# A block's values by way of DRAM, and another order of a turn, in a recurrent megakernel

## The chip, the cores and the metric

The kernel runs on one core of one Trainium2 chip. The metric is device time in microseconds of one execution, the median of several runs. A core has five engines that work side by side, each through its own instructions in order: TensorE (PE, matmuls and transposes into PSUM; PEld is its weight load), VectorE (DVE), ScalarE (ACT), GpSimd (POOL) and SyncE (SP), which here issues nearly all DMAs. They wait for each other only through semaphores.

## The reference

The input is 16 sequences of 256 tokens with 128 features. It is normalized, and goes two ways that meet at the end, `out = x + s * silu(g)`:

- `s`: a small state-space layer. Two convolutions of four taps, a softplus step size, and a scan over the 256 tokens for each of 16 states, `h = dA * h + d * u * B`, `y = sum over states of h * C`, then a projection.
- `g`: six layers, each of an attention and a feed-forward part with residuals. Both read the tokens with half of the features shifted by one token.

```python
def attn_layer(x, Wqkv, qs, ksc, Wo):          # 16 heads of 64
    q, k, v = split(x @ Wqkv)
    q = l2norm(q) * qs;  k = l2norm(k) * ksc
    q = q * cos * scale + rotate_half(q) * sin * scale
    k = k * cos / scale + rotate_half(k) * sin / scale
    # windows of 32 queries: each sees its own 32 keys and the 32 before them
    sim  = einsum(bq, look(bk)) * 8;  sim = where(mask, -big, sim)
    out  = einsum(softmax(sim), look(bv))
    return out @ Wo

def ffn_layer(x, g, bln, W1, b1, W2, b2):      # 128 -> 2 * 341 -> 128
    a, gate = split((layernorm(x) * g + bln) @ W1 + b1)
    return (a * gelu(gate)) @ W2 + b2
```

The diff bears on `look(bv)`: to each window of 32 queries belong 64 rows of values, its own 32 and the 32 before, so that each row of values is wanted in two places.

## The kernel before

Activations stay in SBUF in fp32 as `xT` (features on partitions). Attention works in blocks of 128 tokens: 2 blocks per sequence (`blk` 0 and 1), 32 per layer, 192 over the six layers. A block passes through a pipeline, and a program loop takes one **turn** per block. In turn `n` the tuple `order` is walked, and a pair `(step, ahead)` works on block `n + ahead`: `project 4` projects q and k of block `n + 4`, `scale 2` and `turn 2` normalize and transpose those of block `n + 2`, `score 1`, `greatest 1`, `subtract 1`, `soften 1` and `values 1` make the softmax's numerators and the values of block `n + 1`, and `turn_weights 0`, `attend 0`, `divide 0`, `turn_out 0` finish block `n`. `close` applies Wo to a whole sequence, in two halves of 8 matmuls: the first at the end of an odd turn, the second in the next even one. `guess`, `refine`, `close` and `residual` run for odd blocks only.

Into these turns other work is fed:

- `feed` advances the feed-forward part of an earlier group of four blocks by one step, three times in a turn; a group of 512 tokens takes four turns. By n mod 4: turn 1 transposes the tokens and takes row statistics (L162 and L163 on VectorE, `rstd` on GpSimd), turn 2 normalizes (GpSimd's `less`, four ScalarE activations) and transposes back, turn 3 runs 12 hidden matmuls (L359) with gelu, turn 0 the 6 of the second product (L382) and two residual adds (L385). After the last layer, `end` closes a group in a turn 0: silu on ScalarE, a product on VectorE, 4 transposes (L411), a sum, the output's DMA.
- `state` advances the scan by one of 16 states: `decay` (ScalarE exp), `drive` (GpSimd), `advance` (VectorE scan, L298), `weigh` (GpSimd, two products) and `bring` (on SP, the DMA that broadcasts two rows of 512 for the state after next, 512 KB; its three buffers make it wait for `weigh` of the same turn). A group of 512 tokens takes 20 turns; all eight are through by about turn 165. `prepare` computes the next group's inputs, `norms_on` the first normalization of later groups.

The order of the instructions on each engine is the order of the program (`manual_schedule`). So a step late in `order` that waits on its engine holds up all steps behind it on that engine, in the next turn too. The framework puts in the semaphores: for data, and for reuse of a buffer.

PSUM is one tile of 8 banks of 512 floats; `where` gives each step's first bank. A name read by `pair` takes two banks, one read by `bank` takes one: pairs are q, k, v, qT, kT, s (scores), w (transposed weights), av (attention results of heads 0 to 6), o (its transposes), h0 to h2 (hidden products); single banks are e and l (results of the last heads), pw (Wo), f and n.

The values: `values` projects them into PSUM, and `hand_out` copies them with ScalarE into `vt` (L490), 128 tokens by 2 x 8 heads of 65 floats, the 65th of each head being 1, for the softmax's denominator. From there DMAs on SP place each window's 64 rows in `v2`, one copy per parity `r` of the head, and `attend` multiplies by those rows:

```python
nc.tensor.matmul(
    b["pav7"][r][jj, 0:VW] if c == 7 else b["pav"][jj, r, c, :],
    aT[rr, c, jj],
    v2[rr, j, c * VW : (c + 1) * VW], ...
```

`attend` starts with the pair of heads 7, whose results lie in banks e and l, and `divide_last` divides them; `divide` divides the rest.

Of the kernel before, what the change touches and what calls it, by code (L numbers as in the profile page):

```python
# [8 lines left out]
FP = mybir.dt.float32  # L9
# [6 lines left out]
B, L, DM = 16, 256, 128  # L16
NT = B * L
DEPTH = 6
H, DH, W = 16, 64, 32
NP = H // 2  # L20
# [6 lines left out]
VW = DH + 1  # L27
# [3 lines left out]
def tile_kernel(ctx: ExitStack, tc: tile.TileContext, a, out):  # L31
    nc = tc.nc
# [4 lines left out]
    p = ctx.enter_context(tc.tile_pool(name="at", bufs=1))  # L37
    ff = ctx.enter_context(tc.tile_pool(name="ff", bufs=1))
    mb = ctx.enter_context(tc.tile_pool(name="mb", bufs=1))
    far = ctx.enter_context(tc.tile_pool(name="far", bufs=2, space=bass.MemoryType.DRAM))  # L40
    pst = ctx.enter_context(tc.tile_pool(name="pst", bufs=1, space=PSUM))


    where = dict(q="6", k="0", v="4", qT="4", kT="0", s="2", w="4", av="2", o="2", h0="6", h1="0", h2="4", e="7", l="6", pw="4", f="7", n="1")
    psum = pst.tile([128, 8, G], FP, name="psum")

    def pair(name):
# [369 lines left out]
    blocks = [dict(layer=n // BL, s=n % BL // NB, blk=n % NB) for n in range(DEPTH * BL)]  # L417

    vts = [const.tile([128, 2, NP, VW], FP, name=f"vt{i}") for i in range(NB)]
    v2s = [const.tile([128, 4, NP * VW], FP, name=f"v2{i}") for i in range(NB)]  # L420
    kTs = [const.tile([128, NP, W + L], FP, name=f"kT{i}") for i in range(2)]
    for t in vts:
        nc.gpsimd.memset(t[:, :, :, DH : DH + 1], 1.0)
    for o in (0, 64):
        nc.gpsimd.memset(v2s[0][o : o + W, 0, :], 0.0)
    for t in kTs:
        nc.gpsimd.memset(t[:, :, 0:W], 0.0)

# [56 lines left out]
    def hand_out(n):  # L485
        b = blocks[n]
        blk, pq = b["blk"], b["pv"]

        vt = vts[blk]
        nc.scalar.copy(  # L490
            vt[:, :, :, 0:DH].rearrange("p r c d -> p c r d"),
            pq.rearrange("p (c r d) -> p c r d", c=NP, r=2),
        )
        vt = vt.rearrange("p r c d -> p r (c d)")

        v2 = v2s[blk]
        for r in range(2):
            o = r * 64
            if blk:
                before = vts[blk - 1].rearrange("p r c d -> p r (c d)")  # L500
                nc.sync.dma_start(out=v2[o : o + W, 0, :], in_=before[96:128, r, :])
            nc.sync.dma_start(out=v2[o + W : o + 64, 0, :], in_=vt[0:W, r, :])
            for j in range(1, 4):
                nc.sync.dma_start(
                    out=v2[o : o + 64, j, :], in_=vt[W * (j - 1) : W * (j + 1), r, :]
                )

    def lengths(n, i):
# [252 lines left out]
    def feed():  # L761
# [5 lines left out]


    order = (
        (norms_on, None),  # L770
        (lengths, 3, 1),
        (guess, 3),
        (close, -1, 1),
        (residual, -1),
        (feed, None),
        (project, 4, 0),
        (prepare, None),
        (score, 1),
        (rotate, 4, 0),
        (turn_weights, 0),  # L780
        (rotate2, 4, 0),
        (greatest, 1),
        (state, None, weigh),
        (refine, 3),
        (subtract, 1),
        (scale, 2, 0),
        (turned_weights, 0),
        (project, 4, 1),
        (square, 4, 0),
        (state, None, bring),  # L790
        (values, 1),
        (scale, 2, 1),
        (add, 4, 0),
        (rotate, 4, 1),
        (state, None, decay),
        (hand_out, 1),
        (rotate2, 4, 1),
        (add, 4, 1),
        (attend, 0),
        (divide_last, 0),  # L800
        (state, None, drive),
        (turn, 2, 0),
        (divide, 0),
        (state, None, advance),
        (square, 4, 1),
        (lengths, 4, 0),
        (turned_q, 2),
        (feed, None),
        (feed, None),
        (state, None, put_out),  # L810
        (turn_out, 0),
        (turned_out, 0),
        (turn, 2, 1),
        (turned_k, 2),
        (close, 0, 0),
        (soften, 1),
    )
    last = DEPTH * BL - 1
    with tc.manual_schedule():
# [125 lines left out]
```

## Time and profile before

| | us |
|---|---|
| median of 3 runs | 3457.33 |
| lowest and highest | 3450.86, 3460.79 |
| the profiled execution's own time | 3454.1 |
| its span, first to last instruction | 3452.3 |

| engine | busy, us | share |
|---|---|---|
| PE | 3280.4 | 95% |
| DVE | 2758.3 | 80% |
| POOL | 2592.6 | 75% |
| ACT | 2135.5 | 62% |

The DMA engines moved 305 MB, 88 GB/s; their packets took 33.1% of the time of 16 engines on SP's queue. The mean granted TensorE clock was 0.987. In lists of groups and of the timeline, a line names the start, the duration, the engine, the kernel's line (L437), the operation, what is written and read, and in brackets how long the engine stood idle before, and who released it.

### The profile page before, as it was taken

Reading aid. Unit: us, or ns where it says so; the run is one execution under the profiler, and the core shown is the slowest. Engines: PE = TensorE matmul, PEld = TensorE weight load, DVE = VectorE, ACT = ScalarE, POOL = GpSimd, SP = SyncE. Lnnn points to the kernel's source line nnn. Section 1 sums busy time; section 2 is a strip of 40 time slices with the busy share of each in tenths; the row PEclk is TensorE's granted clock in tenths of the full one; section 3 lists DMA queues with packets and bytes.
Section 4 is the critical chain, followed back from the end, with each engine's and each line's share of the span. In section 5 each row is a group of like instructions: output and inputs, shape, how many; then the busy total and the mean of one; then the engine's idle time right before and its main releaser. Section 6 shows DMA issues by size and latency. Waiting matters only on the chain.

```text
span 3452.3 us, 139990 instructions
## 1 busy us (share of the span) xinstructions
PE 3280.4 (95%) x62176; PEld 2186.9 (63%) x62176; DVE 2758.3 (80%) x3642; ACT 2135.5 (62%) x2741; POOL 2592.6 (75%) x2362
## 2 busy tenths in 40 slices
PE   7999999999999999999999999999999999999996
PEld 3666666666666666666666666666666666666664
DVE  6787878887888788878977898778979887677663
ACT  4666666665766576657655666566656666656654
POOL 6688858885888689868986798679968996555550
PEclk9999999999999999999999999999999999999998
DMA  3434333433333333333333333334323332222221
GB/s 93 109 92 107 82 81 99 103 85 82 103 94 92 90 101 96 84 85 91 108 87 88 91 99 88 86 94 100 96 76 98 98 100 70 69 62 67 69 66 56
DMA packets 191850, 305.03 MB, mean 88 GB/s; under 512 B 32719, under 2 KB 58637, under 8 KB 191245
## 3 DMA queue, kind: packets, MB, share of 16 engines
q1 hardware_dynamic: 190956, 295.74, 33.1%
q8 instruction: 489, 8.01, 1.0%
q14 instruction: 117, 0.95, 0.1%
q10 hardware_dynamic: 288, 0.33, 0.0%
HBM read 95.33 MB, written 8.91 MB: 30 GB/s over the span
## 4 chain that ended last, share of the span: by engine, by line
PE 79%; DVE 8%; ACT 5%; issue 3%; POOL 3%; DMA 0%; SPq 0%; DVEq 0%; POOLq 0%; ACTq 0%
PE psum L437 25%; PE psum L562 14%; PE psum L718 10%; PE psum L667 8%; PE psum L359 7%; PE psum L611 6%; PE psum L382 3%; ACT oT L566 3%; DVE o L691 2%; PE psum L597 2%; PE psum L231 2%; DVE hs L298 1%; DVE t L469 1%; DVE ss L514 1%; POOL t L480 1%
## 5 line engine op out<-in xcount | busy, mean ns | idle before, releaser
L480 POOL TENSOR_TENSOR t<-t,t 128x1024 f32<-128x1024 f32 x384 | 958.8, 2506 | 359.6 <-DVE den L683 210.3
L437 PE MATMUL psum<-wqkv,xT 128*128 128x512 f32 x2304 | 1067.8, 599 | 9.0 <-ACT aT L566 5.0
L552 POOL TENSOR_TENSOR t<-t,y 128x1024 f32<-128x1024 f32 x384 | 722.6, 1903 | 7.5
L437 PEld LDWEIGHTS psum<-wqkv,xT 128*128 128x128 f32 x2304 | 418.3, 192 | 391.7 <-issue 308.7
L458 DVE TENSOR_TENSOR t<-psum,tab 128x1024 f32<-128x1024 f32 x384 | 468.4, 1220 | 161.4 <-PE psum L437 150.7
L566 ACT COPY aT<-psum 128x1024 f32<-128x1024 f32 x192 | 194.3, 1012 | 563.9 <-PE psum L562 563.9
L469 DVE TENSOR_TENSOR t<-psum,tab 128x1024 f32<-128x1024 f32 x384 | 466.4, 1215 | 0.0
L514 DVE TENSOR_REDUCE ss<-sq 128x16 f32<-128x1024 f32 x384 | 456.6, 1199 | 1.3
L562 PE MATMUL psum<-ident,t 128*128 128x128 f32 x3072 | 412.6, 277 | 21.8 <-issue 9.8
L667 PEld LDWEIGHTS psum<-v,aT 64*32 64x32 f32 x24576 | 295.2, 105 | 177.2 <-issue 127.3
L448 ACT ACTIVATE sq<-psum 128x1024 f32<-128x1024 f32 x384 | 394.9, 1028 | 15.5 <-DVE t L469 10.8
L718 PE MATMUL psum<-oT,wo 128*128 128x256 f32 x1536 | 357.5, 386 | 24.2 <-ACT oT L566 24.1
L562 PEld LDWEIGHTS psum<-ident,t 128*128 128x128 f32 x3072 | 340.2, 141 | 43.4 <-issue 14.1
L667 PE MATMUL psum<-v,aT 64*32 64x65 f32 x24576 | 331.8, 227 | 26.2 <-issue 24.6
L718 PEld LDWEIGHTS psum<-oT,wo 128*128 128x128 f32 x1536 | 283.8, 190 | 81.7 <-ACT oT L566 47.0
L490 ACT COPY vt<-psum 128x1024 f32<-128x1024 f32 x192 | 196.1, 1022 | 203.6 <-PE psum L437 203.6
L611 PEld LDWEIGHTS psum<-kT,qT 64*32 64x32 f32 x24576 | 283.9, 105 | 12.1 <-issue 1.7
L611 PE MATMUL psum<-kT,qT 64*32 64x64 f32 x24576 | 287.6, 226 | 2.2 <-issue 2.2
L566 ACT COPY oT<-psum 128x1024 f32<-128x1024 f32 x192 | 195.3, 1017 | 129.8 <-PE psum L562 127.2
L298 DVE TENSOR_TENSOR_SCAN hs<-dA,bc 128x512 f32<-128x512 f32 x128 | 271.5, 2121 | 0.0
L624 DVE TENSOR_REDUCE top<-psum 128x16 f32<-128x1024 f32 x192 | 233.4, 1216 | 46.3 <-PE psum L611 46.2
L359 PE MATMUL psum<-xn,w 128*128 128x512 f32 (+1 forms) x576 | 264.0, 609 | 5.5 <-ACT o L684 4.6
(104 smaller groups left out, 4601.2 us busy)
## 6 DMA issues: line engine op xcount, KB each, us to landing
v<-vt SPq DMA_DIRECT2D x1152, 130.0 KB, 2.4
bc<-rows SPq DMA_DIRECT2D x128, 512.0 KB, 5.1
v<-vt SPq DMA_DIRECT2D x576, 65.0 KB, 2.7
wqkv<-in_Wqkv SPq DMA_DIRECT2D x18, 512.0 KB, 6.5
wo<-in_Wo SPq DMA_DIRECT2D x6, 512.0 KB, 4.2
first<-in_x SPq DMA_DIRECT2D x8, 256.0 KB, 5.0
xn<-xT SPq DMA_DIRECT2D x16, 128.0 KB, 2.7
pad<-xn SPq DMA_DIRECT2D x8, 256.0 KB
```

Source lines behind the costliest of these rows:

```text
L359: nc.tensor.matmul(ph[0:n, i * G : (i + 1) * G], w1[:, i * DI + c0 : i * DI + c0 + n], xn, start=True, stop=True,)
L437: nc.tensor.matmul(pq[:, cc], xb, wq[:, cc], start=True, stop=True)
L458: nc.vector.tensor_tensor(t1.rearrange("p (h d) -> p h d", h=H), b["pq", i].rearrange("p (h d) -> p h d", h=H), table(n, i, 0).unsqueeze(1 ...
L469: nc.vector.tensor_tensor(t2.rearrange("p (h f d) -> p h f d", h=H, f=2), b["pq", i].rearrange("p (h f d) -> p h f d", h=H, f=2)[:, :, ::- ...
L480: nc.gpsimd.tensor_tensor(b["qk", i], b["qk", i], b["t2", i], ALU.add)
L514: nc.vector.tensor_reduce(b["ss"][:, j * H : (j + 1) * H], b["sq", i].rearrange("p (h d) -> p h d", h=H), AX.X, ALU.add,)
L552: nc.gpsimd.tensor_tensor(t3, t3, b["inv"][:, j * H : (j + 1) * H].unsqueeze(2).to_broadcast([128, H, DH]), ALU.mult,)
L562: nc.tensor.transpose(pt[:, cc], of[:, cc], ident)
L566: nc.scalar.copy(to, pt.rearrange("p (c t) -> p c t", c=NP))
L611: nc.tensor.matmul(sc4[jj, r, c, :], qT[rr, c, jj], kT[rr, c, k0 : k0 + 64], start=False, stop=True, skip_group_check=True,)
L667: nc.tensor.matmul(b["pav7"][r][jj, 0:VW] if c == 7 else b["pav"][jj, r, c, :], aT[rr, c, jj], v2[rr, j, c * VW : (c + 1) * VW], start=Tru ...
L718: nc.tensor.matmul(b["pw"][:, 0:L], wo[:, c, :], b["oT"][:, c, :], start=(c == 0), stop=(c == NP - 1), skip_group_check=True,)
```

## The change

It does three things.

- `hand_out` no longer places the windows from `vt`. It writes the block's 128 rows of values, as they are, to a DRAM tile (`vds`, one of two, for even and odd sequences) with one DMA of 520 KB. Ahead of each sequence's first row lie 32 rows of zeros, written once.
- A new step `windows` reads them back into `v2` with four DMAs of 260 KB, for each parity of heads and each half of a window one: 32 partitions by 4 windows by 2080 bytes. It stands at the head of a turn, for the block that the same turn attends.
- `order` is another, and `where` gives other banks. On TensorE the turn was: second half of close, q projection, score, turn_weights, k projection, values, attend, turn q, feed, turn_out, turn k, first half of close. It becomes: turn_weights, second half of close, q projection, score, values, k projection, attend, turn k, turn q, turn_out, feed, first half of close.

```diff
--- before.py
+++ after.py
@@ -41,7 +41,7 @@
     pst = ctx.enter_context(tc.tile_pool(name="pst", bufs=1, space=PSUM))
 
 
-    where = dict(q="6", k="0", v="4", qT="4", kT="0", s="2", w="4", av="2", o="2", h0="6", h1="0", h2="4", e="7", l="6", pw="4", f="7", n="1")
+    where = dict(q="6", k="2", v="0", qT="4", kT="0", s="4", w="2", av="6", o="6", h0="0", h1="2", h2="4", e="4", l="5", pw="0", f="1", n="3")
     psum = pst.tile([128, 8, G], FP, name="psum")
 
     def pair(name):
@@ -421,8 +421,11 @@
     kTs = [const.tile([128, NP, W + L], FP, name=f"kT{i}") for i in range(2)]
     for t in vts:
         nc.gpsimd.memset(t[:, :, :, DH : DH + 1], 1.0)
-    for o in (0, 64):
-        nc.gpsimd.memset(v2s[0][o : o + W, 0, :], 0.0)
+
+    vds = [far.tile([W + L, 2, NP * VW], FP, name=f"vd{i}", bufs=1) for i in range(2)]
+    nc.gpsimd.memset(v2s[0][0:W, 0:2, :], 0.0)
+    for t in vds:
+        nc.sync.dma_start(out=t[0:W], in_=v2s[0][0:W, 0:2, :])
     for t in kTs:
         nc.gpsimd.memset(t[:, :, 0:W], 0.0)
 
@@ -491,18 +494,22 @@
             vt[:, :, :, 0:DH].rearrange("p r c d -> p c r d"),
             pq.rearrange("p (c r d) -> p c r d", c=NP, r=2),
         )
-        vt = vt.rearrange("p r c d -> p r (c d)")
-
-        v2 = v2s[blk]
+
+
+        rows, t0 = vds[b["s"] % 2], blk * 128
+        nc.sync.dma_start(out=rows[W + t0 : W + t0 + 128], in_=vt.rearrange("p r c d -> p r (c d)"))
+
+    def windows(n):
+        b = blocks[n]
+        rows, v2, t0 = vds[b["s"] % 2], v2s[b["blk"]], b["blk"] * 128
         for r in range(2):
-            o = r * 64
-            if blk:
-                before = vts[blk - 1].rearrange("p r c d -> p r (c d)")
-                nc.sync.dma_start(out=v2[o : o + W, 0, :], in_=before[96:128, r, :])
-            nc.sync.dma_start(out=v2[o + W : o + 64, 0, :], in_=vt[0:W, r, :])
-            for j in range(1, 4):
+            for half in range(2):
+                o = r * 64 + half * W
                 nc.sync.dma_start(
-                    out=v2[o : o + 64, j, :], in_=vt[W * (j - 1) : W * (j + 1), r, :]
+                    out=v2[o : o + W],
+                    in_=rows[t0 + half * W : t0 + half * W + 128, r].rearrange(
+                        "(j k) x -> k j x", k=W
+                    ),
                 )
 
     def lengths(n, i):
@@ -767,53 +774,54 @@
 
 
     order = (
+        (windows, 0),
+        (turn_weights, 0),
+        (close, -1, 1),
+        (turned_weights, 0),
+        (project, 4, 0),
+        (lengths, 3, 1),
+        (state, None, decay),
+        (prepare, None),
         (norms_on, None),
-        (lengths, 3, 1),
         (guess, 3),
-        (close, -1, 1),
         (residual, -1),
         (feed, None),
-        (project, 4, 0),
-        (prepare, None),
+        (rotate, 4, 0),
+        (rotate2, 4, 0),
+        (state, None, put_out),
         (score, 1),
-        (rotate, 4, 0),
-        (turn_weights, 0),
-        (rotate2, 4, 0),
+        (square, 4, 0),
         (greatest, 1),
+        (values, 1),
+        (refine, 3),
+        (project, 4, 1),
+        (scale, 2, 1),
+        (hand_out, 1),
+        (scale, 2, 0),
+        (subtract, 1),
+        (attend, 0),
+        (turn, 2, 1),
+        (soften, 1),
+        (divide_last, 0),
+        (rotate, 4, 1),
+        (divide, 0),
+        (add, 4, 0),
+        (square, 4, 1),
+        (rotate2, 4, 1),
+        (turn, 2, 0),
+        (turned_k, 2),
         (state, None, weigh),
-        (refine, 3),
-        (subtract, 1),
-        (scale, 2, 0),
-        (turned_weights, 0),
-        (project, 4, 1),
-        (square, 4, 0),
-        (state, None, bring),
-        (values, 1),
-        (scale, 2, 1),
-        (add, 4, 0),
-        (rotate, 4, 1),
-        (state, None, decay),
-        (hand_out, 1),
-        (rotate2, 4, 1),
+        (turn_out, 0),
+        (turned_out, 0),
+        (state, None, advance),
+        (state, None, drive),
         (add, 4, 1),
-        (attend, 0),
-        (divide_last, 0),
-        (state, None, drive),
-        (turn, 2, 0),
-        (divide, 0),
-        (state, None, advance),
-        (square, 4, 1),
+        (turned_q, 2),
         (lengths, 4, 0),
-        (turned_q, 2),
         (feed, None),
         (feed, None),
-        (state, None, put_out),
-        (turn_out, 0),
-        (turned_out, 0),
-        (turn, 2, 1),
-        (turned_k, 2),
+        (state, None, bring),
         (close, 0, 0),
-        (soften, 1),
     )
     last = DEPTH * BL - 1
     with tc.manual_schedule():
```

## The prediction

> **What bounds the kernel now.** I read the page's busy times and chain first.
>
> ```profile
> PE 3280.4 (95%) x62176; PEld 2186.9 (63%) x62176; DVE 2758.3 (80%) x3642; ACT 2135.5 (62%) x2741; POOL 2592.6 (75%) x2362
> PE 79%; DVE 8%; ACT 5%; issue 3%; POOL 3%; DMA 0%; SPq 0%; DVEq 0%; POOLq 0%; ACTq 0%
> ```
>
> TensorE is busy 95% of the span and carries 79% of the chain; DMA carries 0% of it. The list of TensorE's own waits shows how little could be gained:
>
> ```profile
> PE psum L411 <- DVE xn L407: 39.1, 8, 6.0
> PE psum L718 <- ACT oT L566: 24.1, 95, 1.1
> ```
>
> (Total us, times, longest.) Eight closing steps wait 39 us, the Wo product 24 us; nothing else that an order could mend is over 10 us. Last I read one cycle of four turns in the timeline (start, us, engine, line). I name a turn by n mod 4: the feed-forward steps make 2 short (normalizing), 3 long (12 hidden matmuls), 0 middling, 1 short.
>
> ```profile
> 2405.87 0.41 PE L597 MATMUL psum<-mask,ident_h 64*32 64x512 bf16 x8
> 2415.13 3.07 DVE L298 TENSOR_TENSOR_SCAN hs<-dA,bc 128x512 f32<-128x512 f32 x1
> ...
> 2417.08 1.88 PE L437 MATMUL psum<-wqkv,xT 128*128 128x512 f32 x4
> ...
> 2418.89 0.41 PE L597 MATMUL psum<-mask,ident_h 64*32 64x512 bf16 x8
> ...
> 2420.37 1.21 DVE L458 TENSOR_TENSOR t<-psum,tab 128x1024 f32<-128x1024 f32 x1
> ...
> 2423.97 1.23 DVE L634 TENSOR_TENSOR at<-psum,top 128x1024 f32<-128x1024 f32 x1
> ...
> 2425.03 1.70 PE L667 MATMUL psum<-v,aT 64*32 64x65 f32 x128
> ...
> 2434.47 1.01 ACT L566 COPY oT<-psum 128x1024 f32<-128x1024 f32 x1 [0.19 <-PE psum L562]
> 2435.53 3.72 PE L718 MATMUL psum<-oT,wo 128*128 128x256 f32 x16 [0.23 <-ACT oT L566]
> ```
>
> The score starts at 2405.87, 2418.89, then 2440.90 and 2455.68: turns of 13.02, 22.01, 14.78 us. TensorE runs these back to back. VectorE is up to 1.3 us behind (L458 at 2420.37, though its projection began at 2417.08 and the same read comes 1.99 us after the start where VectorE is free, 1505.94 to 1507.93), and it costs nothing: L634's subtract ends at 2425.20, after attend has begun.
>
> **The change, part by part.** TensorE's instructions stay the same, so its work does: transposes of eight 0.88 (0.93 after a change of tile), a projection 1.72, score 1.62, values and k projection 3.53 to attend's start, attend 1.62, half of close 1.72. Only waits can move.
>
> *1. Banks, subtract to attend.* Attend's first results (heads e, l) went to banks 7 and 6, free long before; now they go to 4 and 5, the score's own banks, which subtract reads. Attend must wait for subtract, and between score and attend only values and the k projection are left: 1.62 + 3.53 = 5.15 us from score's start. VectorE needs, from rotate's start, 4.85 (1507.93 to 1512.78) and a signal of 0.06; rotate starts 0.18 after score: 5.09. Margin 0.06, so each lateness of VectorE beyond it is now TensorE's. Laid on the subtract ends of turns 7 to 170, the lateness averages 0.56 (turn 3), 0.01 (0), 0.13 (1), 0.07 (2): 41 × 0.77 = 31 us, the lower end. The new order makes VectorE later: after subtract it stands at divide_last until attend has begun (A + 0.59, as 3359.16 to 3359.75), and rotate k comes only then. From A: 0.59 + 0.25 + rotate 1.13 + divide 1.28 + rotate2 1.13 + scan 2.12 + lengths 1.13 = A + 7.6. TensorE's turn ends at A + 4.76 in turn 2, so the next starts 2.84 late; an odd turn bears 7.89 (attend) − 4.91 − 1.15 (lengths) = 1.83: attend of turn 3 waits 1.0. Turn 0: A + 9.1 with two residual adds against A + 6.89, 2.2 late: 0.4 in turn 1. Turn 1 (A + 9.2 with the statistics, against A + 7.3) leaves 1.9; an even turn, whose projection ends 1.72 later, bears 4.64 − 1.15 − 0.7 (guess) − 0.86 (residual) = 1.93. Turn 3 is long and clears it. 1.4 a cycle × 41 cycles × 0.78 (128 scans in 164 turns) = 45 us. Were every scan as long as the 3.07 above, it would be 4.2 a cycle, 134 us. I take 45: the mean of 2.12 holds such scans already.
>
> *2. Values through DRAM.* Removed per block: 8 or 10 transfers on SP, 0.6 us of issue each. Added: one write of 520 KB, four reads of 260 KB. Their nearest rows:
>
> ```profile
> v<-vt SPq DMA_DIRECT2D x1152, 130.0 KB, 2.4
> bc<-rows SPq DMA_DIRECT2D x128, 512.0 KB, 5.1
> s<-y SPq DMA_DIRECT2D x8, 256.0 KB, 2.7
> 1523.50:1524.00 0.50, 0.33 (x2) 0.30 (x3) 0.50 (x2) 0.50 (x2) 0.00 (x0) 1.00 1.02 172
> 1524.00:1524.50 0.50, 0.50 (x4) 0.45 (x3) 0.50 (x1) 0.50 (x1) 0.00 (x0) 1.00 1.04 180
> ```
>
> (The last numbers are DMA share and GB/s: engines full at 172 to 180; slices with SBUF sources reach 200 to 221.) The write, by s, lands in some 3.7 us; 1.06 MB of reads at 190 GB/s take 5.6 and 1.75 of latency (2.4 less 130 KB at that rate): 7.4 us. On SP the reads queue behind the write's landing and behind bring, which waits until GpSimd's weigh has freed its buffer. Mostly there is time: hand_out ends near 8 us into a turn, the write lands by 13, the reads by 21, attend follows at 22 or later. Not from turn 2 to 3. There GpSimd starts late, held by turn 1's row statistics (VectorE has them 2.1 into turn 2): 1.3 (rstd), 0.5 (less), refine 3.87, two scales 3.75, add 2.35, the first half of weigh 1.27: bring goes at 15.4, 0.9 into turn 3. Then 512 KB and 1.06 MB: 0.9 + 1.75 + 8.3 = 10.95, where part 1 has attend at 8.9: 2 us. At 259 GB/s (295.74 MB over 33.1% of the span, the mean while busy) they land at 8.75 and it is nothing. I take the half, 1 us, in the 27 cycles with weigh and bring (0.65 of 41): 27 us, ends 0 and 60.
>
> The Trainium skill (DMA: Bandwidth & Descriptors, "Anatomy of one DMA") gives about 2.0 us and the bytes over 436 GB/s for one transfer; bc lands in 5.1 us, not the 3.2 of that estimate. By the rule the reads would land before 7 and this term be nothing.
>
> *3. Close and turn_out.* The second half of close moves behind turn_weights; the first waits for oT 2.15 after turn_out's start (1.08 + 1.02 + 0.05, as at 2434.47). Today one turn of eight lies between, a wait of 0.39; then in turn 3 twelve matmuls (−0.39), in turn 1 four transposes: 0.8 (+0.43). 48 × 0.04 = 2 us. turn_out writes banks 6 and 7, where divide reads: free at A + 3.4, wanted at A + 3.43. Jitter costs 0 to 20, I take 6.
>
> *4. Ends.* In the eight closing steps soften no longer stands before the silu and its table load, but turn and turn_out no longer cover: from the end of the last product 0.2 + 1.5 (adds) + 1.3 + 0.8 = 3.9 of wait, now 5.4 (3371.62 − 3366.2). −1.5 × 8 = −12; ends −30 and 0. In the last turns, with no projection to hide them, the reads come some 5 us later than now (3 to 10). TensorE's unexplained issue waits (25 us in L667) may grow with the traffic, 0 to 10, taken 5.
>
> *5. At nothing.* Refine, scales and turns: scale q ends at 11.7 in turn 2, turn q wants it at 12.3; should GpSimd slip by 1 us there, 0.4 × 41 = 16 us. Turn_weights at the head of a turn: soften is done near A + 1.1, the k banks it overwrites are free at A + 4.5, before the turn's end. Values wait for residual (bank 0): 4.9 against 6.08. Weigh and drive move behind add q on GpSimd: the scan takes last turn's drive, landed 10 us earlier, so only bring feels it (part 2). The other issues on SP that move with their steps (put_out's s, prepare's pad, z and rows, the norms' xn, Wqkv and Wo) come once in 20 or 32 turns, now behind the reads; each has a turn to land, and one that waits for ScalarE holds up the next write by 1 or 2 us of its 8. Decay moves up on ScalarE, in a place where it has nothing ready before values. Two zero writes at the start sit behind loads.
>
> Sum: 45 + 27 + 8 + 5 + 5 − 12 = +78 on the profiled 3454.1 (span 3452.3 and 1.8 around it): 3532; the median lies 3 us higher: 3535 us.
>
> **The rivals.** (a) *VectorE keeps up* and the holes close: attend's wait stays under 0.1 a cycle, the reads land in time, so parts 1 and 2 fall away, and what remains is −12 at the ends, −19 in turn 3's close without turn 1's +20, if ScalarE's copy comes sooner: 3457 − 31 = 3426. For it: TensorE waits only on 62 us today. Against it: the margin of 0.06 and the late turns that the trace already has. It decides if VectorE's lateness at turn 3 stays below 1.83. (b) *The loads are the bound*: reads at 170 GB/s or behind a later bring hold attend in turns 1 and 3, 2 us each, 41 × 0.78 × 4 = 128 on top of 45 − 4: 3626. For it: 1.6 MB queued at once at a rate that the trace has at 180. Against: bring is early in three turns of four. (c) *Nothing moves*: the waits added equal those closed, 3450 to 3467.
>
> **How the numbers follow.** 0.3% (10 us) is about what a measurement of this kernel tells from no change. My case has 0.55, (a) 0.2, (b) 0.15, (c) 0.1. The lower ends, 31 + 0 + 2 + 3 − 30, give 3463, the upper, 134 + 60 + 22 + 20, give 3693; half of (a) and most of (b) inside: 3440 to 3630. Faster: (a), 0.2; same: (c), 0.1; slower: 0.7.
>
> **What would show it.** Right: L667 waits for subtract (L634), most in the turns after the normalizing one, 30 to 90 us in all; SP's longest waits are the reads'; L718's wait moves into turn 1; L411's falls. Wrong: no L634 wait on L667, or one on the v reads above 80 us, or turn_weights waiting for soften or rotate2.

## The result, and the profile after

The changed kernel takes 3669.44 us, the kernel before, run beside it, 3455.04: a ratio of 1.0612 [1.0587, 1.0637]. So it is slower, as forecast, but by 214 us and not by 78, and the time lies above the range. The closest case is rival (b).

The page of the changed kernel (busy times, instruction queue, shares of the chain, DMA issues with KB and median us to landing); L674 is attend's matmul, L569 the transposes, L618 the score, L440 a projection, L725 close, L508 the reads, L500 the write, L280 bring:

```profile
span 3655.0 us, 138188 instructions
PE 3304.3 (90%) x62176; PEld 2218.3 (61%) x62176; DVE 2668.6 (73%) x3642; ACT 2150.2 (59%) x2741; POOL 2593.1 (71%) x2361
q8 instruction: 489, 8.01, 1.0%
PE 77%; DMA 7%; issue 5%; DVE 4%; ACT 3%; POOL 2%; SPq 1%; POOLq 0%; DVEq 0%; ACTq 0%
v<-vd SPq DMA_DIRECT2D x768, 260.0 KB, 7.2
vd<-vt SPq DMA_DIRECT2D x192, 520.0 KB, 3.2
bc<-rows SPq DMA_DIRECT2D x128, 512.0 KB, 6.6
```

DMA, at 0% of the chain before, now carries 7%, and the share in which TensorE waited for nothing that the profile shows ("issue") went from 3% to 5%. TensorE's list of waits (us in all, times, longest) had these entries for attend (L667) and the transposes (L562) in before:

```profile
PE psum L667 <- issue: 24.6, 22, 2.6
PE psum L562 <- issue: 11.2, 9, 3.8
```

and no wait for v. In after it begins so:

```profile
PE psum L674 <- DMA v<-vd: 75.1, 42, 3.7
PE psum L674 <- issue: 71.6, 41, 3.5
PE psum L569 <- issue: 42.4, 30, 3.1
PE psum L725 <- ACT oT L573: 32.5, 49, 1.1
PE psum L618 <- issue: 30.5, 21, 2.6
PE psum L411 <- DVE xn L407: 28.7, 8, 4.4
PE psum L440 <- issue: 12.3, 4, 4.5
PE psum L674 <- DVE at L641: 7.4, 11, 1.2
```

Summed over the whole list, the span's +203 us are: waits named "issue" from 40 to 159 (+119), waits for the reads from 0 to 75 (+75), busy time +24, other waits −10, and holes of under 0.15 us, which the list leaves out, −5.

*The waits for the reads* fall in one turn of four: 66 of the 75 us are in turns 3 (36 pieces of 42; sorted by the score's start). One such turn, behind the attend of the turn before it (start, us):

```profile
1080.80 1.54 PE L674 MATMUL psum<-v,aT 64*32 64x65 f32 x128
1084.35 1.29 POOL L291 TENSOR_TENSOR hs<-bc,hs 128x512 f32<-128x512 f32 x1
1085.38 1.04 PE L569 MATMUL psum<-ident,at 128*128 128x128 f32 x8
1085.66 0.38 SPq L280 DMA_DIRECT2D bc<-rows  x1
1086.13 3.16 SPq L508 DMA_DIRECT2D v<-vd  x4
1088.36 1.46 PE L618 MATMUL psum<-kT,qT 64*32 64x64 f32 x128
1089.75 3.70 PE L440 MATMUL psum<-wqkv,xT 128*128 128x512 f32 x8
1094.81 0.27 PE L674 MATMUL psum<-v,aT 64*32 64x65 f32 x2 [1.36 <-DMA v<-vd]
1097.86 2.06 PE L674 MATMUL psum<-v,aT 64*32 64x65 f32 x126 [2.78 <-DMA v<-vd]
```

This is the chain that part 2 described: weigh's first product (L291) ends at 1085.64 and lets bring go, the reads follow on the same queue, and attend, whose turn comes at 1093.4, gets its first rows at 1094.8 and the last at 1097.8. The place was right (turn 2 to 3). From bring's issue until attend goes on with the last rows it is 12.2 us here, where the sum had 10. This turn is one of the slow ones: over 31 such turns between 10 and 165 the last packet of the reads ends 11.0 us (median) after bring's issue.

*The waits named "issue"* come in bursts, most of them with the reads in flight:

```profile
1460.11 0.38 SPq L280 DMA_DIRECT2D bc<-rows  x1
1460.58 2.86 SPq L508 DMA_DIRECT2D v<-vd  x4
1460.72 1.94 PE L440 MATMUL psum<-wqkv,xT 128*128 128x512 f32 x4
1462.59 0.41 PE L604 MATMUL psum<-mask,ident_h 64*32 64x512 bf16 x8
1462.82 1.46 PE L618 MATMUL psum<-kT,qT 64*32 64x64 f32 x128
1468.75 5.76 PE L440 MATMUL psum<-wqkv,xT 128*128 128x512 f32 x8 [4.47 <-issue]
```

The projections behind the score stand for 4.47 us, though the profile shows nothing that they wait for. The page says what it may be: queue 8, "instruction", moved 8.01 MB in 489 packets, 16.4 KB each, and TensorE's program has 125,161 instructions, 256 for each packet. In the trace's records of that queue, laid beside TensorE's instructions, 89 of the 92 "issue" waits of over 0.3 us stand at one position modulo 256 (193 or 194), and TensorE goes on 1.2 to 1.6 us (median 1.4) after a packet has landed, in before as in after. A packet takes 1.0 us (median) before and 1.2 after; what changed more is when it starts: counted from TensorE's step into the instructions loaded before, 1.5 us at the 75th and 3.1 at the 90th percentile before, 3.4 and 4.9 after. Score (264 instructions in under 2 us) and attend (256 in 1.5) each use up 256 instructions faster than the next can come. Gaps of over 0.3 us at such boundaries, whatever they are put down to: 35 before, 41 us in all, and 96 after, 163 us.

The Trainium skill (Runtime: NRT & Kernel Launch, "Instruction fetch mechanics") has instructions come in 16 KiB blocks of 256, and calls the cost of crossing into the next "mostly hidden". The block size agrees with the 16.4 KB a packet; "hidden" does not hold here, where 159 us of the span are such waits.

*The clock* adds to both. The trace records the granted TensorE clock, and in these runs it is whole or half. It stood at half for 91 us in before and for 242 in after, in 48 stretches; all but the last, which the end of the run cuts, are 3.41 us or a multiple of it long, and each begins within 7 us of the start of a wait of 1.7 us or more. In the turn above, before the score and after the long wait (start:end, us; busy time of PE, PEld, DVE, ACT, POOL; granted clock; DMA share; GB/s):

```profile
1460.72:1462.66 1.94, 1.94 (x14) 0.70 (x19) 1.94 (x3) 1.94 (x3) 1.94 (x2) 1.00 0.46 130
1468.75:1473.00 4.25, 4.25 (x6) 1.67 (x6) 0.00 (x0) 0.64 (x1) 4.25 (x3) 0.50 0.17 37
```

The eight projections at 1468.75 take 5.76 us, those at 1089.75 took 3.70, and attend's last 126 matmuls at 1097.86, at half clock too, take 2.06, where all 128 took 1.54 a turn before; from start to start of such matmuls it is 853 ns (median) at half clock and 429 else. Half of the added 150 us is 75 us; counting only the time in which TensorE was busy at half clock (63 and 193 us), 65. So the +24 of busy time are an added 65 to 75 from the clock, less 31 that attend saves (last section), less 10 to 20 whose place is open. That the waits bring the clock down is read from their order; no run changed the clock alone.

### The profile page after: what moved, and what is told of

Same layout as the page of the kernel before. It is cut to its first block, busy times and chain, and to the rows that moved or that the text cites. A ratio compares the mean times of both kernels' runs of the same rounds, so it can differ in the third digit from the quotient of the medians.

```text
span 3655.0 us, 138188 instructions
## 1 busy us (share of the span) xinstructions
PE 3304.3 (90%) x62176; PEld 2218.3 (61%) x62176; DVE 2668.6 (73%) x3642; ACT 2150.2 (59%) x2741; POOL 2593.1 (71%) x2361
## 3 DMA queue, kind: packets, MB, share of 16 engines
q8 instruction: 489, 8.01, 1.0%
## 4 chain that ended last, share of the span: by engine, by line
PE 77%; DMA 7%; issue 5%; DVE 4%; ACT 3%; POOL 2%; SPq 1%; POOLq 0%; DVEq 0%; ACTq 0%
PE psum L440 22%; PE psum L569 19%; PE psum L725 9%; PE psum L674 8%; PE psum L359 7%; DMA v<-vd 7%; PE psum L618 5%; PE psum L382 3%; ACT oT L573 1%; PE psum L604 1%; PE psum L231 1%; SPq L508 1%; POOL t L559 1%; PE psum L189 1%; DVE t L472 1%
## 5 line engine op out<-in xcount | busy, mean ns | idle before, releaser
L483 POOL TENSOR_TENSOR t<-t,t 128x1024 f32<-128x1024 f32 x384 | 979.1, 2550 | 468.6 <-DVE t L472 247.1
L440 PE MATMUL psum<-wqkv,xT 128*128 128x512 f32 x2304 | 1097.3, 612 | 17.3 <-issue 12.3
L440 PEld LDWEIGHTS psum<-wqkv,xT 128*128 128x128 f32 x2304 | 421.6, 193 | 423.9 <-issue 387.6
L674 PEld LDWEIGHTS psum<-v,aT 64*32 64x32 f32 x24576 | 281.5, 108 | 313.5 <-issue 207.4
L674 PE MATMUL psum<-v,aT 64*32 64x65 f32 x24576 | 326.1, 234 | 154.5 <-DMA v<-vd 75.1
L569 PE MATMUL psum<-ident,t 128*128 128x128 f32 x3072 | 419.0, 293 | 45.8 <-issue 36.0
L569 PEld LDWEIGHTS psum<-ident,t 128*128 128x128 f32 x3072 | 366.3, 150 | 70.3 <-issue 42.5
L725 PE MATMUL psum<-oT,wo 128*128 128x256 f32 x1536 | 369.7, 384 | 34.0 <-ACT oT L573 32.5
L725 PEld LDWEIGHTS psum<-oT,wo 128*128 128x128 f32 x1536 | 281.3, 191 | 100.4 <-ACT oT L573 44.1
L618 PE MATMUL psum<-kT,qT 64*32 64x64 f32 x24576 | 285.8, 225 | 30.6 <-issue 30.5
L618 PEld LDWEIGHTS psum<-kT,qT 64*32 64x32 f32 x24576 | 279.2, 105 | 44.6 <-issue 34.3
L573 ACT COPY kT<-psum 128x1024 f32<-128x1024 f32 x192 | 194.5, 1013 | 121.9 <-PE psum L569 121.7
```

The lines of the kernel that those rows point to most:

```text
L440: nc.tensor.matmul(pq[:, cc], xb, wq[:, cc], start=True, stop=True)
L483: nc.gpsimd.tensor_tensor(b["qk", i], b["qk", i], b["t2", i], ALU.add)
L569: nc.tensor.transpose(pt[:, cc], of[:, cc], ident)
L573: nc.scalar.copy(to, pt.rearrange("p (c t) -> p c t", c=NP))
L618: nc.tensor.matmul(sc4[jj, r, c, :], qT[rr, c, jj], kT[rr, c, k0 : k0 + 64], start=False, stop=True, skip_group_check=True,)
L674: nc.tensor.matmul(b["pav7"][r][jj, 0:VW] if c == 7 else b["pav"][jj, r, c, :], aT[rr, c, jj], v2[rr, j, c * VW : (c + 1) * VW], start=Tru ...
```

## The experiments

Four theories were on the table: the order and banks cost the time (part 1 of the prediction); the reads arrive late, behind bring (part 2; theory Q in the later expectations); the write to DRAM costs it; the reads hold up TensorE's instruction loads (theory B), a cause that the prediction had at 5 us. Of each run: time, ratio to before with its interval, then from its profile the waits named "issue", those for the transfers of values (v, vd), TensorE's busy time and its time at half clock (us), and how many instruction loads started over 3 us after TensorE's step into the 256 instructions loaded last. The profiles of f1, f2 and f3 are of runs 15 to 26 us above the median, that of after is 13 below it.

| run | us | ratio | issue | values | busy | half clock | late |
|---|---|---|---|---|---|---|---|
| before | 3455 | 1 | 40 | 0 | 3280 | 91 | 55 |
| after | 3669.4 | 1.0612 [1.0587, 1.0637] | 159 | 75 | 3304 | 242 | 143 |
| e1 order only | 3460.4 | 1.0022 [1.0006, 1.0038] | 41 | 1 | 3290 | 81 | 10 |
| e2 transfers only | 3496.3 | 1.0133 [1.0113, 1.0154] | 93 | 7 | 3270 | 132 | 78 |
| e3 no reads | 3387.4 | 0.9812 [0.9792, 0.9832] | 29 | 0 | 3224 | 77 | 26 |
| e4 no writes | 3678.4 | 1.0655 [1.0634, 1.0677] | 156 | 82 | 3317 | 272 | 120 |
| e5 sixteen reads | 3720.2 | 1.0763 [1.0665, 1.0862] | 119 | 61 | 3406 | 258 | 69 |
| e6 eight partitions | 3936.4 | 1.1389 [1.1304, 1.1474] | 113 | 247 | 3383 | 507 | 66 |
| e7 reads before bring | 3564.7 | 1.0313 [1.0226, 1.0401] | 143 | 5 | 3271 | 153 | 79 |
| e8 half the reads | 3465.5 | 1.0031 [1.0018, 1.0044] | 60 | 26 | 3248 | 118 | 69 |
| e9 e2, bring late | 3607.5 | 1.0441 [1.0419, 1.0464] | 171 | 18 | 3299 | 200 | 122 |
| g1 reads for nobody | 3547.4 | 1.0269 [1.0246, 1.0293] | 140 | 0 | 3267 | 156 | 96 |
| g2 the same from SBUF | 3491.9 | 1.0099 [1.0071, 1.0128] | 104 | 0 | 3258 | 129 | 103 |
| g3 short bring | 3652.9 | 1.0572 [1.0549, 1.0596] | 152 | 65 | 3321 | 276 | 120 |
| f1 before, 2 windows direct | 3445.7 | 0.998 [0.9961, 1.0] | 59 | 0 | 3275 | 112 | 60 |
| f2 e1, 2 windows direct | 3440.1 | 0.9961 [0.9943, 0.9978] | 45 | 0 | 3283 | 97 | 8 |
| f3 e7, 2 windows direct | 3535.6 | 1.0237 [1.0195, 1.028] | 134 | 2 | 3293 | 207 | 28 |

### The two halves of the change

**e1**: the new `order` (without `windows`) and `where`, with the transfers of before.

```diff
-        (windows, 0),
...
+        v2 = v2s[blk]
+        for r in range(2):
...
```

> The changed kernel's order of a turn and its banks, with the transfers of the kernel before (vt to v2 within SBUF, 8 or 10 a block). After the change TensorE waits 157 us for its own instructions (39 before) and 75 us for the value reads (0 before). Theory T, the traffic: instruction fetches and reads are late because of the DRAM transfers, so without them the instruction waits fall to 40 to 60 us, the waits for v to under 5 us, and the time to 3450 to 3490 us. Rival O, the order and the banks: attend on subtract, and fewer matmuls between the instruction-heavy score and attend, cause it; then the time stays above 3600 us with over 120 us of instruction waits.

The time moved by 0.2%. TensorE's waits:

```profile
PE psum L718 <- ACT oT L566: 33.1, 49, 1.1
PE psum L411 <- DVE xn L407: 30.0, 8, 4.7
PE psum L667 <- DVE at L634: 8.2, 9, 1.7
```

Close's and the ends' waits are as in after. Attend's wait for subtract (L634) is 8.2 us, where part 1 had 45. Part 1 had carried over the scan's 2.12 us; VectorE's groups, of before and then of e1, show that this did not hold (busy us, mean ns):

```profile
L298 DVE TENSOR_TENSOR_SCAN hs<-dA,bc 128x512 f32<-128x512 f32 x128 | 271.5, 2121 | 0.0
```

```profile
L298 DVE TENSOR_TENSOR_SCAN hs<-dA,bc 128x512 f32<-128x512 f32 x128 | 184.0, 1437 | 0.0
```

What counts is what GpSimd is running when a scan starts. In before 127 of the 128 start while one of its products runs, and end 1.08 us after that product (the scan's length and the product's rest correlate at 0.9999). The 3.07 us scan in the prediction's timeline, started at 2415.13, stands beside this row of before, two `add`s, of which the first ends at 2417.1:

```profile
2414.76 5.62 POOL L480 TENSOR_TENSOR t<-t,t 128x1024 f32<-128x1024 f32 x2
```

In after 61 scans start with no product running, most of them just ahead of an `add`; such a scan takes 1.21 us, and the `add` 3.15, where it takes 2.34 alone:

```profile
2427.74 1.21 DVE L298 TENSOR_TENSOR_SCAN hs<-dA,bc 128x512 f32<-128x512 f32 x1
2427.96 3.15 POOL L483 TENSOR_TENSOR t<-t,t 128x1024 f32<-128x1024 f32 x1 [0.19 <-DVE t L472]
```

In e1 104 scans meet a running product, but on average 0.40 us before its end, and not 1.05 as in before. No run changed this alone.

With 1.44 in place of 2.12 the working of part 1 gives attend of turn 3 a wait of 0.3 us and turn 1 none: 0.3 × 41 × 0.78 = 10 us, near the 8.2. But 6.9 of the 8.2 us are in turn 1 and 1.0 in turn 3, so the nearness is luck.

**e2**: the order and banks of before, with the new transfers, `windows` at the head of the turn.

```diff
     order = (
+        (windows, 0),
         (norms_on, None),
```

> The order and the banks of the kernel before, with the changed kernel's write to DRAM and four reads (windows at the head of a turn). Theory T: most of the loss is here, instruction waits of 100 us or more and some 20 to 75 us for v: 3560 to 3660 us. Rival O: 3450 to 3480 us, instruction waits near 40 us.

+42 us, which neither expectation had; the issue waits grow by 53, the reads' wait is 7. So order alone (+6) and transfers alone (+42) are far from the +214 of both together.

### What of the transfers

**e3**: reads for the first two blocks only. **e4**: writes for the first four only. **e8**: after the first two blocks, the reads of one parity `r` only.

```diff
     def windows(n):
+        if n >= 2:          # e3
+            return
```
```diff
+        if n < 4:           # e4
             nc.sync.dma_start(out=rows[W + t0 : W + t0 + 128], ...
```
```diff
-        for r in range(2):
+        for r in range(2 if n < 2 else 1):          # e8
```

> The changed kernel with the four reads left out after the first two blocks, so that every block attends to the first blocks' values; the write of each block remains. Theory T: no waits for v (75 us gone) and instruction waits down from 157 to 60 to 90 us: 3480 to 3530 us. Rival D, that the waits put down to instruction issue are waits on something else in the order: they stay near 150 us, and only the 75 us go: 3590 us.

> The changed kernel with the write of a block's values to DRAM left out after the first four blocks; the four reads remain and bring old rows. Theory T: the reads go out earlier, as nothing is waited for, so waits for v fall below 30 us; instruction waits fall by the write's share, some 45 of 157 us: 3560 to 3600 us. Rival D: instruction waits stay near 150 us: 3600 to 3640 us.

> The changed kernel with only two of the four reads after the first two blocks: the odd heads of a pair (r = 1) attend to the first blocks' values. No reads at all gave 3387 us, all of them 3669. Theory B: a fetch is held by what is queued, which halves with the reads, and a wait of half the length is mostly hidden: 3420 to 3490 us. Rival R, in proportion to the bytes: 3528 us, 3500 to 3560.

The write costs nothing (+9 us without it: both expectations missed). e3 lies below both of its expectations: the reads cost 3669.4 − 3387.4 = 282 us, and half of them 78 (e8, as theory B had it): the second half costs 204. Between e3's profile and after's, the span grows by 267: issue waits +130, waits for values +75, busy +80 (68 to 83 of it the clock: 242 us at half for 77), the rest −19. Without reads the new order is 73 us below e1, so the SBUF transfers of before also have their price, and the 214 us of the change are 282 − 68.

**e5**: sixteen reads of 65 KB for four of 260, each 32 partitions by one window. **e6**: sixteen, each 8 partitions by four windows.

```diff
+                for j in range(4):          # e5
+                    k0 = t0 + half * W + j * W
+                    nc.sync.dma_start(out=v2[o : o + W, j, :], in_=rows[k0 : k0 + W, r])
```
```diff
+                for q in range(4):          # e6
+                    o = r * 64 + half * W + 8 * q
+                    nc.sync.dma_start(out=v2[o : o + 8], in_=rows[...].rearrange("(j k) x -> k j x", k=W)[8 * q : 8 * q + 8])
```

> The changed kernel with the same bytes read in sixteen transfers of 65 KB instead of four of 260 KB. In the traces TensorE crosses into a new block of 256 instructions at fixed places, each crossing starts a 16 KB fetch on the DMA engines, and every long gap there ends 1.25 to 1.6 us after such a fetch; over 3 us pass from crossing to the fetch's start 143 times of 483 after the change, 55 before. Theory B, the burst: a fetch waits behind all that a read has queued on its DMA engine, so reads that are handed over in small pieces at SP's pace let it in sooner: late fetches under 70, 3480 to 3560 us. Rival R, the rate: any 1 MB of reads from DRAM in a turn delays them, however it is cut: over 120 late fetches, above 3620 us.

> As e5 in count and size of reads, but each read fills 8 partitions for all four windows instead of 32 partitions for one. By the Trainium skill (DMA: Bandwidth & Descriptors, 'Why a DMA increments its semaphore by 16 and not by 1') such a transfer runs on 8 DMA engines, which leaves half of them free for fetches; no run has shown this yet. Theory B with free engines: fewer late fetches than e5 if fetches are spread over all engines, 3450 to 3540 us, but the reads take longer to land (over 9 us), so waits for v may pass 100 us. Rival R: as in e5, above 3620 us.

Both missed in time. In e5 fewer loads start late (69 for 143) and the issue waits fall by 40, but SyncE needs 10.5 us (median) to issue a block's reads, where after needs 2.6:

```profile
2413.11 12.10 SPq L510 DMA_DIRECT2D v<-vd  x16
```

and TensorE's busy time grows by 102, hardly by the clock (258 us at half for 242): attend, from its first to its last start, takes 507 us in sum and not 404, presumably since its matmuls wait row by row for what lands. In e6 the waits for values grow to 247 (319 with those of attend that the profile puts down to other transfers, though attend reads nothing else that a DMA brings), and the time at half clock to 507, with hardly fewer late loads than in e5.

### Why the two halves together cost more than their sum

**e7**: the reads of the next block go ahead of bring at the end of the turn. **e9**: e2 with bring moved to the end of the turn, so that it stands ahead of the reads.

```diff
-        (windows, 0),
...
+        (windows, 1),
         (state, None, bring),          # e7
```
```diff
-        (state, None, bring),
...
+        (state, None, bring),
     )                                   # e9
```

> The changed kernel with windows moved from the head of the turn to the end of the turn before, ahead of bring on SP. My prediction had the 75 us of waits for v come from bring, which holds the reads until GpSimd's weigh is done and puts 512 KB ahead of them. If so they fall under 20 us: 3580 to 3620 us, instruction waits unchanged near 150 us. If the waits come from the landing of the write instead, they stay above 50 us and the time above 3640 us.

> e2 (order and banks of the kernel before, value transfers of the changed kernel, 1.3% slower) with bring moved from the middle of a turn to its end, so that its 512 KB stand ahead of the reads on SP, as in the changed order. Moving the reads ahead of bring took 105 us off the changed kernel. Theory Q, the queue: bring ahead of the reads is what makes order and transfers worse together (205 us) than apart (6 and 42): 3540 to 3600 us here, with waits for v of 40 us or more. Rival: the new order's packing of attend and score is what makes reads costly; then bring's place does little here: 3485 to 3515 us.

e7 takes 105 us off the changed kernel, more than expected, e9 adds 111 to e2, somewhat more than theory Q had. So the place of bring on the queue makes about half of the loss, from both sides. In e7 the reads land sooner, and the wait for them is nearly gone:

```profile
v<-vd SPq DMA_DIRECT2D x768, 260.0 KB, 4.8
PE psum L674 <- DMA v<-vd: 5.2, 2, 3.0
```

The issue waits fall by 16 only, from 159 to 143; busy time falls by 33, with 153 us at half clock for 242.

In e9 the 111 us are mostly issue waits (+78) and busy time (+30, at half clock 200 us for 132), waits for values only +11, where theory Q had 40 or more.

**g3**: bring left at its place, but after the first group of 512 tokens it moves 64 of 512 columns.

```diff
-                out=bc[n + 2], in_=of[g]["rows"][:, n + 2, :].partition_broadcast(128)
+                out=bc[n + 2] if g == 0 else bc[n + 2][:, :, 0:64],
...
```

> The changed kernel, but after the first group of 512 tokens the broadcast of the scan's two rows moves only their first 64 columns (64 KB and not 512 KB); the scan uses what its three buffers hold. Theory Q (the 105 us that moving the reads ahead of this broadcast saved are its bytes, 512 KB ahead of the reads on one queue): v waits under 15 us, waits without a releaser 90 to 140, 3530 to 3580. If the instruction loads feel the sum of the bytes in flight, somewhat less still, 3480 to 3530. Rival (what counts is that SyncE stands at the broadcast until GpSimd frees its buffer, and the reads are issued late): v waits stay over 50 us, 3630 to 3670.

Taking away seven eighths of bring's bytes in seven groups of eight saves 16 us of the 105, and the rival's numbers hold:

```profile
PE psum L676 <- DMA v<-vd: 64.5, 36, 3.4
SPq L281 <- POOL hs L293: 353.4, 96, 8.0
```

SyncE waits at bring's issue for GpSimd's weigh, up to 8.0 us, and the reads behind it go late. By the issue rows of the timeline (turns 10 to 165), between the end of an attend and the next read's issue lie 1.1, 2.3 and 3.8 us at the 50th, 75th and 90th percentile in after, 1.2, 2.4 and 3.8 in g3, and 1.1, 1.2 and 1.3 in e7. So it was for the most part bring's wait, not its bytes. (The short broadcast still lands in 5.9 us, the long one of e7 in 6.5. But its packets are gone: those of 256 and 2048 bytes, which the broadcasts and some weights make up, took 382 us of the 16 engines' time in after and 93 in g3, and yet from bring's issue to the reads' last packet, in turns 2 to 3, it is 10.1 us in g3 for 11.0.)

### Late arrival or held-up instruction loads

**g1**: the reads go as in after, but into a tile that nobody reads; attend takes the first block's rows throughout. **g2**: the same, the four transfers taken from SBUF.

```diff
-        rows, v2, t0 = vds[b["s"] % 2], v2s[b["blk"]], b["blk"] * 128
+        rows, v2, t0 = vds[b["s"] % 2], v2s[1 if n else 0], b["blk"] * 128
...
-        aT, v2 = b["aT"], v2s[b["blk"]]
+        aT, v2 = b["aT"], v2s[0]
```
```diff
-                    in_=rows[t0 + half * W : t0 + half * W + 128, r].rearrange(...)
+                    in_=v2s[0][o : o + W] if n else ...          # g2
```

> All blocks' values are attended from the first block's rows (attend reads v2 of block 0 throughout), and every read of a later block goes as in the changed kernel, at the same place, but into the second v2, which nobody reads. So the reads move the same bytes from DRAM and no instruction of TensorE waits for one. The kernel without reads took 3387.4 us, the changed kernel 3669.4. Theory B (the reads hold up TensorE's own instruction loads): the waits without a releaser stay at 100 to 160 us over all of TensorE's lines, the time is 3520 to 3600, and over 80 of the loads start more than 3 us after TensorE has passed into the last loaded block. Rival L (the reads cost only because attend waits for them): no v wait is left, the waits without a releaser are under 40 us, the time is 3380 to 3410.

> As the kernel whose reads nobody waits for, but after the first block the four transfers of 260 KB take their rows from SBUF (the first v2, 32 partitions to 32 partitions) and not from DRAM. Theory D (it is the DRAM source that holds up the instruction loads, which come from DRAM too): waits without a releaser 20 to 45 us, 3385 to 3420. Theory T (any 1 MB moved at that place does): the same as with the reads from DRAM, within 15 us.

Waits named "issue" of e3 (L571 and L676 are its transposes and attend), then of g1, then of g2:

```profile
PE psum L571 <- issue: 24.6, 19, 2.5
PE psum L676 <- issue: 2.9, 2, 2.0
```

```profile
PE psum L674 <- issue: 90.3, 44, 3.4
PE psum L618 <- issue: 23.8, 18, 2.6
PE psum L569 <- issue: 17.9, 16, 2.7
PE psum L440 <- issue: 7.5, 3, 3.1
```

```profile
PE psum L674 <- issue: 61.0, 39, 3.1
PE psum L569 <- issue: 25.8, 18, 2.9
```

g1 against e3 is the cleanest pair of the study: TensorE's programs differ by 2 instructions in 124,793, and no matmul waits for a read in either. 160 us lie between them. By the profiles the span grows by 153, issue waits by 111 and busy time by 43, all else by nothing; the 43 are the clock's, at half for 156 us and 77 (half of the difference is 40). Of the issue waits over 0.3 us, those that began no later than 8 us after a read's issue sum to 0 in e3 and 108 in g1, the others to 29 and 31. So the reads cost 160 us though nobody wants them, and theory B's numbers hold; late arrival, with what the clock adds to it, has the other 3669.4 − 3547.4 = 122.

g2 lands between its two theories: +105 over e3. So 1 MB in four transfers at that place holds up the loads from SBUF too (103 late, 96 in g1); from DRAM it costs 55 us more. Where the instructions themselves are loaded from, no run shows.

### Fewer transfers

For two pairs of (parity, window) the 64 rows lie in `vt` on the partitions where attend wants them. **f1**, **f2** and **f3** let attend read those from `vt` and do not move them: in the kernel of before, in e1, and in e7.

```diff
+                if j == 1 + 2 * r:
+                    continue
...
-                        v2[rr, j, c * VW : (c + 1) * VW],
+                        (vt[rr, r] if j == 1 + 2 * r else v2[rr, j])[:, c * VW : (c + 1) * VW],
```

> The kernel before, but attend reads two of the eight windows (r = 0, j = 1 and r = 1, j = 3) straight from vt, where they already lie on the right partitions; two of 8 or 10 transfers go. If transfers cost TensorE time through late instruction fetches and through the waits within attend (1.48 us with 8 or 10 transfers, 1.32 with four): instruction waits fall from 39 to 25 to 35 us, attend to 1.44, 3420 to 3445 us. If the transfers of the kernel before cost nothing, as its profile suggested to me: 3450 to 3460 us.

> e1 (the new order and banks with the transfers of the kernel before, 3460 us) with the same two windows read straight from vt. With no reads from DRAM at all the new order ran in 3387 us, and attend took 1.72 us in e1 against 1.32 there. If it is the number of transfers that attend waits for: 3410 to 3440 us. If not: 3450 to 3460 us.

> e7 (the changed kernel with the reads ahead of bring, 3565 us) with the same two windows straight from vt: three quarters of the bytes are read, in six transfers. Half of the bytes gave 3465 us with bring still ahead. Theory B, a fetch held by what is queued: 3470 to 3520 us and late fetches (over 3 us from crossing to start) down from 79 to 60. If the number of reads counts more than their bytes: above 3550 us.

f1 lies between its two expectations, and 6 us below before is within the noise. f2, the new order and banks with the old SBUF transfers less two, is the fastest of the kernels that do all of the work, by 0.4% below before (0.2 to 0.6%). f3 missed: six reads of three quarters of the bytes save 29 us on e7, with intervals that overlap, and 134 us of issue waits stay, although only 28 loads start over 3 us late. So that count alone does not tell the cost; the gaps at the boundaries sum to 146 us in f3.

## Why the prediction was right and wrong

- **Part 1, attend waits for subtract, 45 us (31 to 134).** Wrong: 7.4 in after, 8.2 in e1. The step that failed is the scan's 2.12 us, taken over from a place where GpSimd's `add` is running when the scan starts to one where it takes 1.44 (1.49 in after). The lower end of 31, laid on the subtract ends of before, failed with it, and so did the first test under "What would show it", 30 to 90 us of L634 waits. The place was wrong too: turn 1 has 5.3 of the 7.4 us, and turn 3, which was to have most, 1.7; why was not followed.
- **Part 2, values through DRAM, 27 us (0 to 60).** The mechanism was right: bring held by weigh, the reads behind it, in turn 3 after turn 2, and the 75.1 us of read waits are the largest wait that attend has. The size was off. A wait of 2 us a cycle was worked out and half of it taken, for 27 cycles; measured are 66 us in 24 turns 3, 2.8 each. So to halve it was the larger error, and the landing was 1 us later than the sum (11.0 us after bring's issue for 10). The rule of the skill set beside it, by which the term would be nothing, was further off: bc lands in 6.6 us in after, not 3.2. The section cited has that fit for transfers that GpSimd issues; these SyncE issues. It also had one price for lateness, the wait for the rows. The place behind bring costs 105 us in all (e7); by the profiles, 98 us apart, these are 70 of waits for values, 16 of issue waits and 33 of busy time, less some 20 by which other waits are longer in e7.
- **Part 4, issue waits "may grow with the traffic, 0 to 10".** The term that broke the forecast: +119 in waits, and more by the clock. The 25 us in L667 were seen and left unexplained. g1 puts the whole at 160 us over a kernel without reads. Rival (b) had the right side, "the loads are the bound", and for the wrong engine's share: it charged 128 us to data that is late, in turns 1 and 3, where 122 are that (of the waits for values themselves, 66 of 75 us in turn 3) and 160 are TensorE's own program, held up. It came within 43 us by chance: it also had 41 for part 1, and it counted from before, where the 282 count from a kernel 68 us faster.
- **Part 3, close.** The sign of each turn was right: turn 3's wait went from 10.7 us to 1.1, turn 1's from 12.3 to 31.4. The net was +8.4 and not +2, since turn 3 had 10.7 to lose and not 48 × 0.39 = 19. The other 6, for turn_out behind divide, do not appear (o L698: 3.0 us, 4.1 before). That the sum of 8 fits is luck.
- **Part 4, ends.** Right: L411 fell from 39.1 to 28.7, forecast −12; the reads' waits in the last turns are 7.4 us, forecast 5.
- **Part 5, at nothing.** No wait for soften or rotate2 appears; SP's other issues cost nothing that these lists show.
- **"TensorE's instructions stay the same, so its work does."** This step failed as well: it put the clock at nothing. 242 us at half clock for 91 make TensorE's work 65 to 75 us longer; only 24 show, as attend got shorter.
- **Rival (a)** had VectorE right (its wait stayed small) and e1 is that case without the transfers; it still was 6 us slower and not 31 faster. **Rival (c)**, 3450 to 3467, is where e1 lies.
- **The range** failed since its upper end had no case in which the issue waits, in sum the largest wait of before (40 us), move with the traffic, nor one for the clock. The bound of 10 had no row behind it.

Open: why the 8 or 10 SBUF transfers of before, which move the same 1.06 MB a block, hold up so few loads (e1: 10 late, 41 us of waits). They are smaller (130 KB, 2.5 us to land) and stand at another place in the turn; e5's smaller reads lowered the late loads to half only. By what rule a load waits for the data queue was not shown either, only that it starts later.

## What to carry to other kernels

A TensorE program of many small matmuls is itself a stream of loads: where 256 instructions run in 1.5 us, as here, waits that the profile puts down to "issue" can be a price of DMA traffic, and a change that gathers transfers in front of the densest matmuls is to be charged for it, even where the data come in time. A forecast of long waits is to be charged for the clock too: here 65 to 75 us on 194 us of added waits. Look where on its queue a moved transfer stands, and what the instruction ahead of it waits for: here moving the reads past one waiting issue was worth 105 us, taking that issue's bytes away 16. A duration measured behind one neighbour is not carried to a place behind another; the scan here went from 2.12 to 1.44 us.

## What the runs showed of the hardware that was not expected

- TensorE's instructions come in packets of 16.4 KB for 256 instructions, and its long "issue" gaps stand at their boundaries. It goes on 1.2 to 1.6 us after the landing, at the median 1.4, in before and in after.
- Each stretch at half clock in after follows a wait of 1.7 us or more and lasts 3.41 us or a multiple; 21 of the 26 waits of over 3 us have one behind them.
- A scan that starts while a GpSimd product runs ends 1.08 us after that product; one that starts ahead of it takes 1.21 us, and the product is the longer (3.15 for 2.34 us).
- 1 MB in four transfers that nobody reads costs TensorE 160 us over 190 blocks from DRAM, 105 from SBUF; a 520 KB write to DRAM in the same turn costs nothing (e4).
- Attend, from its first to its last matmul's start, takes 1.48 us (median) with 8 or 10 transfers to wait for (1.72 in e1), 1.43 and 1.55 with two fewer (f1, f2), 1.32 with four, with two (e8) and with none (e3). That saved the changed kernel some 31 us, which the prediction did not have; the cause was not tested.
- Sixteen reads of 65 KB a block cost more with 8 partitions each (e6) than with 32 (e5): 216 us lie between the two kernels.
